# Cross-attention of a decoder layer: scores on four 32-row strips with dense keys, all 16 heads in one run

## The chip, the cores and the metric

The kernel runs on one core of a Trainium2 chip. Its engines are TensorE (PE; matmuls and their weight loads, which the profile shows as PEld), VectorE (DVE), ScalarE (ACT), GpSimd (POOL) and SyncE (SP, which issues most DMA transfers). The kernel keeps operands in SBUF, and PE's results go to PSUM, which the kernel divides into tiles of 128 partitions x 512 floats, a bank each; DVE and ACT read them from there.

The metric is the device time of one execution in microseconds (us), as the median of several runs.

## The reference

One decoder layer on `x` of shape (2, 2048, 512), in three parts, each added to its input and followed by a layer norm:

- a state-space mixer over the sequence (projections, a convolution of four taps, a scan in chunks, an output projection),
- cross-attention of 16 heads of 32 features over a context of 77 tokens for each of the two batches,
- a mixture of 16 slots: slots attend to all tokens (dispatch), each slot goes through its own expert (three matrices of 512 x 2048), and tokens attend to the slots (combine).

The middle part is what the change touches:

```python
q = (x @ q_w + q_b).reshape(B, T, H, D).transpose(0, 2, 1, 3)
k = (context @ k_w + k_b).reshape(B, S, H, D).transpose(0, 2, 1, 3)
v = (context @ v_w + v_b).reshape(B, S, H, D).transpose(0, 2, 1, 3)
att = jnp.einsum('bhtd,bhsd->bhts', q, k) / jnp.sqrt(jnp.float32(D))
causal = jnp.tril(jnp.ones((T, S), dtype=bool))
att = jnp.where(causal[None, None, :, :], att, -jnp.inf)
att = jax.nn.softmax(att, axis=-1)
y = jnp.einsum('bhts,bhsd->bhtd', att, v)
```

The causal mask matters only for the first 77 of 2048 tokens of a batch.

## The kernel before

The program has four stages, one after another, with little overlap between them. Times are of the profiled execution.

1. *Mixer* (0 to about 326 us): projections, convolution and scan. Beside it, in a generator called `setup`, the keys, values and a few folded matrices of the later stages are prepared, a step at a time, where the letter `U` stands in hand-tuned strings of letters (`TUNED["seq"]`).
2. *Attention* (about 326 to 912 us): 16 periods of 256 tokens (8 for each batch).
3. *Experts* (from about 912 us): 16 experts whose weights (192 pieces of 1 MB) stream from HBM through buffers in SBUF.
4. *Combine*: tokens attend to slots, last layer norm, output.

A period of the attention stage handles tokens 256 at a time, in two halves (`s`) of 128. Its pieces are small functions: `load`, `scaled`, `out_proj` (the mixer's output projection, residual and norm), `x1_transposed`, `queries` (in two halves of 256 features), `weigh` (scores and softmax of a group `hg` of four heads), `gather` (transposes the probabilities), `values` (probabilities times values), `o_proj` (output projection, residual, norm), `x2_transposed`, `dispatch`, `p_transposed` and `collect` (attention of the slots). Pieces of different periods are interleaved by a plan of eight steps for a period (`TUNED["plan"]`), where `W`, `G` and `V` stand for the next `weigh`, `gather` and `values`, with lists of their own for the stage's head and drain. That gives the order in which the source issues the work; when the program is built, a scheduler still moves instructions within each engine's queue, and the engines then run their queues in that fixed order.

Most matmuls work on numbers split into a high and a low part of a reduced float32 type (float32r, `FR`), three matmuls for a product: high x high, high x low, low x high. They are recorded by the helper `mm` (line 231); `split` makes the two parts (lines 234 and 242).

*Scores.* The features of four heads fill the 128 partitions, 32 each. The keys of a batch are laid out as block-diagonal matrices `kbh`, `kbl` of 128 x (4 heads x 77): in the columns of head `r` only its own 32 rows are not zero. So one matmul over all 128 rows gives the scores of four heads for 128 tokens, 128 x 308; three of them make a group. The result `sc` takes one PSUM bank, of two that take turns. `setup` writes the block-diagonal layout with four copies of 32 partitions each (`kf`, line 443), for each batch and each half of the features.

*Softmax.* For groups 1 and 3, DVE takes the maximum (line 810), subtracts it (line 811), ACT exponentiates, DVE sums (line 813). For groups 0 and 2, DVE takes the negated maximum (line 815) and ACT exponentiates four times with the maximum as bias and a running sum (line 818). DVE inverts the sum (line 819) and POOL scales (line 820).

*Values.* The probabilities `pp` are transposed on PE (line 828) into a bank `tr` and copied out to `pt`, of which there are three buffers. `values` multiplies: each head takes 32 columns of the PE array (77 rows x 32 columns), four heads side by side, and writes 32 partitions of the bank `y`, which is one bank of its own. Each float32 matmul of this kind is two records. After the fourth group, ACT and DVE split `y` into `yv`.

*PSUM in this stage.* `y` 1 bank, `mm` (projections, dispatch, collect) 2, `tr` (transposes) 2, `sc` 2.

Of the kernel before, what the change touches and what calls it, by code (L numbers as in the profile page):

```python
# [16 lines left out]
S = 77  # L17
NE, FF = 16, 2048
# [205 lines left out]
def tile_decoder(ctx, tc, a, out, dbg=None, upto=9, opt=None):  # L224
# [5 lines left out]
    def mm(o, l, r, start, stop, **kw):  # L230
        return pe.matmul(o, lhsT=l, rhs=r, start=start, stop=stop, **kw)  # L231
# [8 lines left out]
    def split(hi, lo, src, lo_eng=None, hi_eng=0):  # L240
        cp(hi_eng, hi, src)
        (lo_eng or dve).tensor_tensor(lo, src, hi, ALU.subtract)  # L242
# [38 lines left out]
    kbh, kbl = ([kv_[b].tile([128, 4, 4 * S], FR, name=f"kb{t}{b}") for b in range(B)] for t in "hl")  # L281
# [11 lines left out]
    with ExitStack() as st:  # L293
# [121 lines left out]
        def setup():  # L415
# [20 lines left out]
            for b in range(B):  # L436
                for h in range(2):
                    m2 = slice(2 * h, 2 * h + 2)
                    kf = sb.tile([128, 2, 4, S], FP, tag="sw", bufs=2, name="kf")
                    pool.memset(kf, 0.0)  # L440
                    for r in range(4):
                        sr = slice(32 * r, 32 * r + 32)
                        dve.tensor_copy(kf[sr, :, r, :], kst[sr, m2, b * S:b * S + S])
                    split(kbh[b][:, m2].rearrange("p m (r s) -> p m r s", s=S), kbl[b][:, m2].rearrange("p m (r s) -> p m r s", s=S), kf, pool)
                    yield
# [255 lines left out]
    with ExitStack() as st:  # L701
        psb = {tag: st.enter_context(tc.tile_pool(name="b_" + tag, bufs=n, space=PSUM, reuse_waits="tile"))
               for tag, n in (("y", 1), ("mm", 2), ("tr", 2), ("sc", 2))}
# [87 lines left out]
        def weigh(n, s, hg):  # L791
# [6 lines left out]
            qh, ql = ts[n]["q", hg // 2]  # L798
            h4 = slice(hg * 4, hg * 4 + 4)
            sc = PT("sc")  # L800
            for k, (l, r) in enumerate(((qh, kbh[b]), (qh, kbl[b]), (ql, kbh[b]))):
                mm(sc[:, 0:4 * S], l[:, hg % 2, ss], r[:, hg, :], k == 0, k == 2)
            sv = sc[:, 0:4 * S].rearrange("p (r s) -> p r s", s=S)
# [19 lines left out]
        def gather(n, s, hg):  # L823
            pp = ts[n].pop(("pp", s, hg))
            pt = sb.tile([S, 4, 128], FP, tag="pt", bufs=opt.get("pt", 3), name="pt")
            tp = PT("tr")
            for r in range(4):
                pe.transpose(tp[0:S, r * 128:r * 128 + 128], pp[:, r, :], ident)  # L828
            cp(EN.get('g%d' % hg, 1 - hg % 2), pt, tp[0:S, :].rearrange("p (r t) -> p r t", t=128))
            ts[n]["pt", s, hg] = pt  # L830

        def values(n, s, hg):
            b = n // NT
            if hg == 0:
                ts[n]["y", s] = PT("y", bufs=1)
            yp = ts[n]["y", s]
            pt = ts[n].pop(("pt", s, hg))
            for r in range(4):
                h = hg * 4 + r
                mm(yp[32 * r:32 * r + 32, hg * 128:hg * 128 + 128], vt[b][:, 32 * h:32 * h + 32], pt[:, r, :], True, True)  # L840
            if hg == 3:
                yh, yl = hi_lo("yv", [128, 4, 128], 1)
                split(yh, yl, ts[n].pop(("y", s)).rearrange("p (k t) -> p k t", t=128))
                ts[n]["yv", s] = (yh, yl)
# [106 lines left out]
        def needs(f, n, *a_):  # L951
# [9 lines left out]
            if f == "weigh":  # L961
                return [x("queries", a_[1] // 2)]
# [21 lines left out]
        if opt.get("drain"):  # L984
            dr_ = [tuple(o) for o in opt["drain"]]
            assert sorted(dr_) == sorted(ops[-len(dr_):])
            ops[-len(dr_):] = dr_
        for o in ops:
            assert all(d in done for d in needs(*o)), o
            assert o not in done  # L990
            done.add(o)
            fns[o[0]](*o[1:])
# [602 lines left out]
```

## Time and profile before

| | us |
|---|---|
| median of 3 runs (lowest to highest) | 1508.82 (1508.0 to 1513.46) |
| the profiled execution, its time | 1504.8 |
| its span | 1502.8 |
| PE busy | 1348.9 (90%) |
| DVE busy | 910.4 (61%) |
| ACT busy | 616.5 (41%) |
| POOL busy | 447.6 (30%) |

| operation of the attention stage | count | us each |
|---|---|---|
| one of three score matmuls, 128 x 308, record | 384 | 0.30 to 0.39 |
| maximum of a group of scores, DVE | 128 | 0.465 |
| subtracting it, DVE | 64 | 0.468 |
| exponential of one head, ACT, and reading its sum | 256 | 0.327 and 0.207 |
| transposing one head's probabilities, record | 512 | 0.273 |
| a pass of one head's values, record | 1024 | 0.273 |
| copy of transposed probabilities, ACT or DVE | 96, 32 | 0.582, 0.676 |
| splitting `y`, ACT, DVE | 32, 32 | 0.586, 0.691 |

How to read it: a record of PE lasts from the start of a matmul to the modelled end of its pipeline, and the next one starts long before. What a matmul costs its neighbours is the distance from its start to the next start. The views by stretch give the busy time of each engine between two moments; the view of the chain follows the work that ended last back from the end, each step to what released it. L231 is the line of the helper that records every matmul, so PE rows are told apart by the tiles that they write and read. In lines of PE, `128*32` is rows times columns of the weights, and `77x128` the moving operand.

### The profile page before, as it was taken

Reading aid. Unit: us, or ns where it says so; the run is one execution under the profiler, and the core shown is the slowest. Engines: PE = TensorE matmul, PEld = TensorE weight load, DVE = VectorE, ACT = ScalarE, POOL = GpSimd, SP = SyncE. Lnnn points to the kernel's source line nnn. Section 1 sums busy time; section 2 is a strip of 40 time slices with the busy share of each in tenths; the row PEclk is TensorE's granted clock in tenths of the full one; section 3 lists DMA queues with packets and bytes.
Section 4 is the critical chain, followed back from the end, with each engine's and each line's share of the span. In section 5 each row is a group of like instructions: output and inputs, shape, how many; then the busy total and the mean of one; then the engine's idle time right before and its main releaser. Section 6 shows DMA issues by size and latency. Waiting matters only on the chain.

```text
span 1502.8 us, 27725 instructions
## 1 busy us (share of the span) xinstructions
PE 1348.9 (90%) x10442; PEld 992.5 (66%) x10442; DVE 910.4 (61%) x2142; ACT 616.5 (41%) x1683; POOL 447.6 (30%) x496
## 2 busy tenths in 40 slices
PE   7899999988999999999999997858978778889896
PEld 6788889867888888888888874205644534533364
DVE  7997997857778888888887763102211111115597
ACT  5534544525655666565665551101100010105456
POOL 4634543645434444444443311000000000000054
PEclk9999999989999999999999997969999798999998
DMA  9889978993221222322210258999999999999447
GB/s 321 209 198 240 229 200 212 239 282 93 71 57 57 64 57 57 92 71 62 59 37 15 71 179 354 387 415 377 418 419 418 418 419 419 418 421 417 160 157 250
DMA packets 188061, 339.64 MB, mean 226 GB/s; under 512 B 12347, under 2 KB 135739, under 8 KB 163096
## 3 DMA queue, kind: packets, MB, share of 16 engines
q1 hardware_dynamic: 171632, 311.25, 59.9%
q10 hardware_dynamic: 16296, 26.62, 5.1%
q8 instruction: 83, 1.36, 0.4%
q14 instruction: 50, 0.41, 0.1%
HBM read 299.56 MB, written 38.27 MB: 225 GB/s over the span
## 4 chain that ended last, share of the span: by engine, by line
PE 58%; DVE 17%; DMA 17%; ACT 4%; issue 3%; POOL 1%; SPq 1%; ACTq 0%; POOLq 0%; DVEq 0%
PE mm L231 27%; DMA ew<-in_e_W 9%; PE up L231 6%; DMA ew<-in_e_Wg 6%; PE pj L231 5%; PE tr L828 4%; DVE X L530 3%; PE sc L231 3%; PE y L231 2%; PE yac L231 2%; PE gp L231 1%; PE uu L231 1%; DVE C L530 1%; PE tr L721 1%; DMA ut<-Ud 1%
## 5 line engine op out<-in xcount | busy, mean ns | idle before, releaser
L231 PE MATMUL up<-ew,hT 128*32 128x512 f32 x944 | 133.5, 637 | 33.0 <-DMA ew<-in_e_W 30.2
L820 POOL TENSOR_TENSOR pp<-pp,den 128x308 f32<-128x308 f32 x128 | 89.5, 704 | 156.8 <-DVE den L819 104.8
L1176 ACT ACTIVATE sv<-up 128x512 f32<-128x512 f32 x32 | 19.1, 597 | 270.2 <-PE up L231 260.5
L1185 POOL MEMSET aT<- 128x512 f32 x16 | 8.3, 525 | 401.2 <-PE yac L231 399.5
L231 PE MATMUL mm<-xTh,cqh 128*128 128x256 f32 x256 | 76.2, 309 | 31.2 <-ACT xTh L234 31.2
L1235 DVE TENSOR_TENSOR Qc<-mm,vec 128x512 f32<-128x512 f32 x32 | 22.1, 692 | 130.8 <-PE mm L231 125.3
L242 DVE TENSOR_TENSOR xTl<-tr,xTh 128x512 fp32r<-128x512 f32 x32 | 21.3, 688 | 113.3 <-ACT xTh L234 113.3
L231 PEld LDWEIGHTS up<-ew,hT 128*32 128x32 f32 x944 | 26.4, 112 | 94.4 <-issue 56.5
L828 PE MATMUL tr<-cst,pp 128*77 128x128 f32 x512 | 81.0, 282 | 2.0 <-DVE x1Tl L724 1.4
L234 ACT COPY pt<-tr 77x512 f32<-77x512 f32 x96 | 55.6, 582 | 63.2 <-PE tr L828 35.4
L231 PEld LDWEIGHTS mm<-xTh,cqh 128*128 128x128 f32 x256 | 51.4, 207 | 44.8 <-ACT xTh L234 34.7
L818 ACT ACTIVATE pp<-sc,mx 128x77 f32<-128x77 f32 x240 | 75.4, 327 | 11.1 <-DVE mx L815 10.3
L231 PE MATMUL mm<-xTl,cqh 128*128 128x256 f32 x256 | 77.6, 305 | 1.7 <-DVE xTl L242 1.7
L231 PE MATMUL mm<-x1Th,w30h 128*128 128x256 f32 x256 | 76.0, 298 | 2.7 <-ACT x1Th L723 1.5
L231 PE MATMUL mm<-xTh,cql 128*128 128x256 f32 x256 | 75.0, 295 | 0.0
L231 PE MATMUL mm<-x1Tl,w30h 128*128 128x256 f32 x256 | 73.8, 288 | 0.7 <-DVE x1Tl L724 0.7
L231 PE MATMUL mm<-x1Th,w30l 128*128 128x256 f32 x256 | 73.4, 287 | 0.0
L828 PEld LDWEIGHTS tr<-cst,pp 128*77 128x77 f32 x512 | 59.8, 148 | 16.7 <-issue 10.3
L530 DVE SCALAR_TENSOR_TENSOR X<-raw,vec,X 128x256 f32<-128x256 f32 x80 | 66.4, 876 | 5.4 <-ACT X L526 4.9
L231 PE MATMUL yac<-ew,aT 128*32 128x512 f32 x488 | 60.4, 631 | 5.8 <-issue 5.1
L746 POOL TENSOR_TENSOR ut<-ut,fb 128x512 f32<-128x512 f32 x32 | 41.3, 1292 | 76.9 <-DMA ut<-Ud 40.9
L231 PEld LDWEIGHTS mm<-xTl,cqh 128*128 128x128 f32 x256 | 52.0, 203 | 17.6 <-issue 14.2
(376 smaller groups left out, 4307.8 us busy)
## 6 DMA issues: line engine op xcount, KB each, us to landing
ew<-in_e_W SPq DMA_DIRECT2D x119, 1024.0 KB, 15.9
ew<-in_e_Wg SPq DMA_DIRECT2D x60, 1024.0 KB, 13.6
BS<-scrBc SPq DMA_DIRECT2D x48, 256.0 KB, 5.2
CS<-scrC SPq DMA_DIRECT2D x48, 256.0 KB, 6.4
xs<-in_xT SPq DMA_DIRECT2D x32, 256.0 KB, 5.7
xt<-in_x SPq DMA_DIRECT2D x32, 256.0 KB, 2.8
ut<-Ud SPq DMA_DIRECT2D x32, 256.0 KB, 3.5
fb<-fd SPq DMA_DIRECT2D x128, 64.0 KB, 3.1
```

What stands on the lines that cost most here:

```text
L231: return pe.matmul(o, lhsT=l, rhs=r, start=start, stop=stop, **kw)
L234: (act.copy, dve.tensor_copy, pool.tensor_copy)[e](o, i)
L242: (lo_eng or dve).tensor_tensor(lo, src, hi, ALU.subtract)
L530: dve.scalar_tensor_tensor(dst, raw[:, j, 1 + t:1 + t + TB], w4[:, t:t + 1], dst, ALU.mult, ALU.add)
L721: pe.transpose(tp[:, k * 128:k * 128 + 128], src[:, k * 128:k * 128 + 128], ident)
L746: (act, dve, pool)[EN.get('uf', 1)].tensor_tensor(ut, ut, fb, ALU.mult)
L818: act.activation(pp[:, r, :], sv[:, r, :], AF.Exp, bias=mx[:, h:h + 1], accum_out=den[:, h:h + 1])
L820: (act, dve, pool)[EN.get('d%d' % hg, 2)].tensor_tensor(pp, pp, den[:, h4].unsqueeze(2).to_broadcast([128, 4, S]), ALU.mult)
L828: pe.transpose(tp[0:S, r * 128:r * 128 + 128], pp[:, r, :], ident)
L1176: last["silu"] = act.activation(sv, up, AF.Silu)
L1185: pool.memset(aT, 0.0)
L1235: dve.tensor_tensor(Qc[b][:, mp * 2:mp * 2 + 2, t1:t1 + TB], qq, vec[:, V_CQ + mp * 2:V_CQ + mp * 2 + 2].unsqueeze(2).to_broadcast([128, 2 ...
```

## The change

- The keys are stored densely: for a batch, 128 partitions x 4 groups x 80 columns (77 and three of padding, `SP = 80`), 32 partitions a head, with no zeros around. `setup` fills them with one copy for each batch and has two steps fewer.
- The scores of a group come from four matmuls side by side in place of one, each over a strip of 32 rows (one head), 80 columns wide. Strip `r` of every group writes into bank `r` of a tile of four PSUM banks, at column `g * 80`. So a product of a group is 4 x 3 = 12 matmuls in place of 3.
- All 16 heads of 128 tokens are multiplied at once, 48 matmuls, when the first group's `weigh` comes. The other three `weigh` only do the softmax. The tile of four banks has one buffer.
- `values` does nothing for groups 0 to 2 and all 16 heads at group 3. Its result takes a bank of the projections (`mm`), and the bank `y` is gone. `pt` has six buffers in place of three.
- `weigh` needs both halves of the queries, and a loop puts every `weigh` of earlier tokens ahead of the first of later ones.

PSUM in this stage is then `mm` 2 banks, `tr` 2, `sc` 4.

```diff
+SP = 80
...
-    kbh, kbl = ([kv_[b].tile([128, 4, 4 * S], FR, name=f"kb{t}{b}") for b in range(B)] for t in "hl")
+    kbh, kbl = ([kv_[b].tile([128, 4, SP], FR, name=f"kb{t}{b}") for b in range(B)] for t in "hl")
...
             for b in range(B):
-                for h in range(2):
-                    m2 = slice(2 * h, 2 * h + 2)
-                    kf = sb.tile([128, 2, 4, S], FP, tag="sw", bufs=2, name="kf")
-                    pool.memset(kf, 0.0)
-                    for r in range(4):
-                        sr = slice(32 * r, 32 * r + 32)
-                        dve.tensor_copy(kf[sr, :, r, :], kst[sr, m2, b * S:b * S + S])
-                    split(kbh[b][:, m2].rearrange("p m (r s) -> p m r s", s=S), kbl[b][:, m2].rearrange("p m (r s) -> p m r s", s=S), kf, pool)
-                    yield
+                kf = sb.tile([128, 4, SP], FP, tag="sw", bufs=2, name="kf")
+                pool.memset(kf, 0.0)
+                dve.tensor_copy(kf[:, :, 0:S], kst[:, :, b * S:b * S + S])
+                split(kbh[b], kbl[b], kf, pool)
+                yield
...
-               for tag, n in (("y", 1), ("mm", 2), ("tr", 2), ("sc", 2))}
+               for tag, n in (("mm", 2), ("tr", 2))}
+        scp = st.enter_context(tc.tile_pool(name="b_sc", bufs=1, space=PSUM, reuse_waits="tile"))
...
             mx, den = ts[n]["mx", s]
-            qh, ql = ts[n]["q", hg // 2]
             h4 = slice(hg * 4, hg * 4 + 4)
-            sc = PT("sc")
-            for k, (l, r) in enumerate(((qh, kbh[b]), (qh, kbl[b]), (ql, kbh[b]))):
-                mm(sc[:, 0:4 * S], l[:, hg % 2, ss], r[:, hg, :], k == 0, k == 2)
-            sv = sc[:, 0:4 * S].rearrange("p (r s) -> p r s", s=S)
+            if hg == 0:
+                sc = ts[n]["sc", s] = scp.tile([128, 4, 512], FP, tag="sc", bufs=1, name="sc")
+                for g in range(4):
+                    qh, ql = ts[n]["q", g // 2]
+                    for k, (l, r_) in enumerate(((qh, kbh[b]), (qh, kbl[b]), (ql, kbh[b]))):
+                        for r in range(4):
+                            sr = slice(32 * r, 32 * r + 32)
+                            mm(sc[:, r, g * SP:g * SP + SP], l[sr, g % 2, ss], r_[sr, g, :], k == 0, k == 2)
+            sv = ts[n]["sc", s][:, :, hg * SP:hg * SP + S]
...
-            pt = sb.tile([S, 4, 128], FP, tag="pt", bufs=opt.get("pt", 3), name="pt")
+            pt = sb.tile([S, 4, 128], FP, tag="pt", bufs=opt.get("pt", 6), name="pt")
...
         def values(n, s, hg):
+            if hg < 3:
+                return
             b = n // NT
-            if hg == 0:
-                ts[n]["y", s] = PT("y", bufs=1)
-            yp = ts[n]["y", s]
-            pt = ts[n].pop(("pt", s, hg))
-            for r in range(4):
-                h = hg * 4 + r
-                mm(yp[32 * r:32 * r + 32, hg * 128:hg * 128 + 128], vt[b][:, 32 * h:32 * h + 32], pt[:, r, :], True, True)
-            if hg == 3:
-                yh, yl = hi_lo("yv", [128, 4, 128], 1)
-                split(yh, yl, ts[n].pop(("y", s)).rearrange("p (k t) -> p k t", t=128))
-                ts[n]["yv", s] = (yh, yl)
+            yp = PT("mm")
+            for g in range(4):
+                pt = ts[n].pop(("pt", s, g))
+                for r in range(4):
+                    h = g * 4 + r
+                    mm(yp[32 * r:32 * r + 32, g * 128:g * 128 + 128], vt[b][:, 32 * h:32 * h + 32], pt[:, r, :], True, True)
+            yh, yl = hi_lo("yv", [128, 4, 128], 1)
+            split(yh, yl, yp.rearrange("p (k t) -> p k t", t=128))
+            ts[n]["yv", s] = (yh, yl)
...
             if f == "weigh":
-                return [x("queries", a_[1] // 2)]
+                return [x("queries", 0), x("queries", 1)]
...
+        for n in range(N):
+            for s_ in range(2):
+                at_ = ops.index(("weigh", n, s_, 0))
+                for o in [x for x in ops[at_:] if x[0] == "weigh" and (x[1], x[2]) < (n, s_)]:
+                    ops.remove(o)
+                    ops.insert(at_, o)
+                    at_ += 1
```

## The prediction

> **What bounds the kernel now.** I read the page first, then busy time by stage, then the chain that ended last inside the attention stage, then the TensorE records one by one around the operations that change.
>
> Busy time by stage (columns: stretch, length, then busy time of PE, weight loads, DVE, ACT, POOL, granted clock, DMA share, GB/s):
>
> ```profile
> 326.00:420.00 94.00, 85.39 (x616) 72.20 (x615) 74.60 (x185) 51.84 (x177) 45.92 (x45) 0.95 0.38 115
> 420.00:860.00 440.00, 436.41 (x3371) 370.20 (x3370) 356.21 (x952) 265.74 (x890) 186.93 (x196) 1.00 0.20 59
> 860.00:912.00 52.00, 46.13 (x345) 35.52 (x343) 32.65 (x97) 26.33 (x79) 11.25 (x14) 0.98 0.56 205
> 912.00:1502.00 590.00, 484.70 (x3392) 253.21 (x3392) 174.77 (x475) 119.34 (x249) 48.22 (x64) 0.91 0.91 367
> ```
>
> Nearly all of the change lies in the attention stage, 326 to 912 us. In its steady part TensorE (PE) is busy 436 of 440 us at full clock, DVE 81%, ACT 60%. Since pipelined matmuls make "busy" too kind, the chain must confirm it. Between 520 and 562 us the chain is PE alone, in this order (start, length, group):
>
> ```profile
> 523.29 2.30 PE mm L231 x10
> 525.60 0.36 PE y L231 x8
> 525.95 0.59 PE tr L828 x4
> 526.54 0.43 PE sc L231 x3
> 526.98 0.44 PE tr L721 x4
> ...
> 545.47 0.79 PE y L231 x24
> ...
> 560.65 0.35 PE y L231 x8
> ```
>
> From 525.60 to 560.65 is one period of 35.05 us (256 tokens; 16 periods), with no wait for another engine in it. So a microsecond more or less of PE work in this stage is a microsecond of the kernel, and work of other engines is free until it becomes late.
>
> The same chain shows what a change of array shape costs. y (the values) runs on strips of 32 columns, tr and sc on the whole array. One y group (four matmuls, eight records) takes 0.36, three together 0.79, so a group is 0.216 of work and a first one has 0.14 more. The transposes after it take 0.59 instead of 0.44, another 0.15. **A visit to strips costs 0.29 us beyond its work.** The PE records show where:
>
> ```profile
> 603.08 0.28 PE L231 MATMUL mm<-x1Tl,w30h 128*128 128x256 f32 x1
> 603.20 0.28 PE L231 MATMUL mm<-x1Th,w30l 128*128 128x256 f32 x1
> 603.32 0.60 PE L721 MATMUL tr<-cst,x 128*128 128x128 f32 x4
> 603.85 0.42 PE L231 MATMUL y<-pt,vt 77*32 77x128 f32 x8
> 604.20 0.66 PE L828 MATMUL tr<-cst,pp 128*77 128x128 f32 x4
> ```
>
> Four transposes start at 603.32 and need 0.44; y starts at 603.85, so 0.09 of nothing lies before it. Another 0.09 lies behind it, and each side pays a first weight load that nothing covers. The weight queue's waits say the same: it stood with no releaser named
>
> ```profile
> PEld y L231 <- issue: 10.7, 41, 0.4
> PEld tr L828 <- issue: 8.5, 43, 0.2
> ```
>
> The third reading is what a short matmul costs:
>
> ```profile
> 250.10 1.85 PE L231 MATMUL qp<-sqTs,dwq 128*128 128x16 f32 x16
> 251.81 0.36 PE L231 MATMUL op<-cs,cst 128*128 128x1 f32 x2
> ...
> 150.32 0.66 PE L231 MATMUL gp<-CS,BS 96*128 96x128 f32 x4
> 150.82 0.33 PE L231 MATMUL pj<-xh,wi1h 128*128 128x256 f32 x1
> ```
>
> Sixteen qp matmuls with 16 moving columns start within 251.81-250.10 = 1.71 us, 0.107 each: 128 columns of weights set the pace, not the moving columns. gp, in the scores' number type with 128 columns, takes 0.50/4 = 0.125 with its first load.
>
> **The change, part by part.**
>
> *Scores, streaming.* Before: 16 periods x 24 = 384 matmuls of 308 columns, 0.43/3 = 0.143 each, 54.9 us. After: 384 groups of four strips, each strip 32 rows, 128 weight columns, 80 moving columns. No row shows row strips. Lower bound of a group: 0.107 to 0.111, the weight load, with the four side by side. Upper bound: one after another, 4 x 0.107 = 0.43. Column strips are the nearest row: the eight y records of a group fit in 0.36, which four serial ones could not. I take 0.111: 42.6 us, **-12.3**.
>
> *Visits.* Before: y in 104 visits (the scheduler joined some of the 128 groups), 104 x 0.29 = 30.2 us. After, in the order the changed program is built in, values take 78 visits, but the scores are not one run: the scheduler cuts them between projections and transposes into 121 visits, and 34 times goes directly from scores to values or back. A score visit has two changes of shape like y's, plus 0.08 for a first load of 128 rather than 32 weight columns, minus 0.07 since its last group, counted at 0.111, streams only 80 columns (80/256 of 0.12): 0.30. Sum 78 x 0.29 + 121 x 0.30 - 34 x 0.15 (one change shared) = 53.8; **+23.6**. Bounds of a score visit: 0 (row strips next to whole-array work need no gap) and 0.45.
>
> "TensorEngine Tiling (Array Packing)" of the Trainium skill, Key Properties, says that any change of tiling mode drains the array; y shows it for column strips, no row shows it for row strips. "TensorE: Matmul & The Clock Gate" there, Measured speedup vs the span model, gives 3.07 times for four row strips; by that a group would be 4 x 0.143/3.07, an estimate of 0.186, and the sum would be 29 us higher.
>
> *One score tile over four banks, single buffer.* A run now waits until all four softmax groups of the last one are read. In the built order 8.4 to 10 us of PE work lie between the runs. Reading needs on DVE four maxima (0.465) and two subtractions (0.468), 2.8 us, and on ACT eight exponentials with sums (0.327+0.207), 4.3 us. The whole softmax is 8.8 us of DVE and 10.4 of ACT in a period, so other work holds about 81-25 = 56% of DVE and 60-30 = 30% of ACT, and these reads need about 6.4 and 6.1 us: covered, with 2 us to spare. If that cover goes, PE stands with the projections queued behind the scores.
>
> *Values in the projections' two banks.* 32 more tiles take turns there. A next projection now waits for a split of the values: ACT 0.586, then DVE 0.69. In the built order most reuse has 2 us of PE work in front; one, the first output projection of a period behind the last collect, has 1.1 us against a DVE read of 0.7 plus its queue. For both bank edits: between 0 and 1.5 us a period; I take 0.3, near 0 since the covers are mostly longer than the chains, **+5**. The six pt buffers end ACT's wait for y (24.9 us in the steady part), off the path: nothing.
>
> *Setup.* 16 kf copies (8.0 us of DVE, two of them 2.46 and 2.34) become two; ACT loses half of 2.8 us of casts, POOL half of 8.7. The generator has two steps fewer, so the weight loads behind it (v_w, d_Wq, d_WkT, on SP's queue) and their matmuls and the POOL memset move forward past projection work. The two long copies lie on the chain, 4.8 us: gain between 0 (the new, wider copies wait as long) and 5, with 3 either way from the moved SP loads; I take **-3**.
>
> *After the stage.* Smaller tiles let five expert loads instead of four be issued at its start, but before had its fifth at 836 us; 1 MB at 418 GB/s is 2.4 us either way: 0.
>
> Sum: -12.3+23.6+5-3 = +13 (rounded). The profiled execution took 1504.8 us (span 1502.8), so 1518; the median of the runs, 1508.8, lies 4 above it, so I predict **1522**.
>
> **The rivals.**
>
> *Row strips change shape for free (faster).* Place: the 121 score visits. Then -12.3 - 7.6 (values, 26 visits fewer) - 3 + 2 of waits = -21: 1488. It decides from a score visit under 0.30 - 13/121 = 0.19 us. For it: shapes with the full 128 columns may not need what column strips need. Against: both gaps around y, on every visit.
>
> *Strips not side by side.* In pairs, 0.215 a group: 384 x 0.104 = +40, 1562. All serial: +122, 1644. For it: every strip loads 128 weight columns, y's only 32. Against: the y group.
>
> *PE waits for the softmax.* At 1 us in each of 32 runs, 32 in place of 5: 1549. It starts once the last group's maximum is over 2 us late in DVE's queue. Against: DVE's 19% idle.
>
> *The next stage swallows it.* From 912 us DMA is busy 91%; if the expert loads don't wait for the end of the attention, its length is hidden: about 1509. Against: they start at 836 to 925 us, as its buffers come free.
>
> **How the numbers follow.** Chances: the forecast 0.58 (1508 to 1540), free row strips 0.13, serial strips 0.09, softmax waits 0.12, swallowed 0.08. The range leaves out serial strips beyond pairs and what lies past free strips: 1486 to 1563. About 0.5%, 7.5 us, is what a measurement can tell from no change. Faster: 0.13 plus 0.03 from the forecast's low edge, 0.16; same: 0.08 swallowed and 0.11 of the forecast below 1516, 0.19; slower 0.65.
>
> **What would show it.** In the after profile: PE busy throughout 420 to 860 and a period near 36 us; score groups of about 0.11 when several stand together; gaps of 0.09 on both sides of each score visit; sc waits on ACT or DVE small; mm waits on the values' split under 0.5 us. Wrong if a score visit costs under 0.2, a group over 0.2, or PE shows waits of a microsecond before sc.

## The result, and the profile after

The changed kernel takes 1663.1 us (median of 4 runs, 1660.3 to 1667.8), the kernel before on the same chip 1511.1 (1508.0 to 1517.0): 1.101 times as long, 95% interval 1.0985 to 1.1032. The forecast was 1522 with a range to 1563: the sign holds, the size is off by more than ten times, +152 us against +13.

Busy time by stretch of the changed kernel (the bounds are set by hand; stretch, length, then PE, weight loads, DVE, ACT, POOL, granted clock, DMA share, GB/s):

```profile
0.00:320.00 320.00, 287.14 (x2646) 253.77 (x2646) 259.72 (x411) 148.82 (x280) 145.76 (x170) 0.94 0.89 228
420.00:1000.00 580.00, 513.95 (x4397) 420.64 (x4396) 371.10 (x983) 284.97 (x921) 191.35 (x198) 0.91 0.15 45
1062.00:1658.00 596.00, 489.27 (x3401) 254.96 (x3399) 176.84 (x486) 121.14 (x255) 48.25 (x64) 0.92 0.90 365
```

Taken between the same events of both profiles: the first transposes of x, with which the attention stage's own work begins, start at 334.7 us instead of 327.2. From there to the last matmul of `collect` it takes 737 us instead of 590, and what follows takes 587 instead of 586. So nearly all of the loss lies in the attention stage. Before, PE was busy 436 of 440 us there at full clock; now it is busy 514 of 580, and the clock granted is 0.91. A period of 256 tokens takes 46 us instead of 35.4.

What PE waited for in that stretch (total us, times, longest; the weight loads, PEld, wait for the same things):

```profile
PEld tr L831 <- POOL pp L823: 39.1, 27, 2.3
PE tr L831 <- POOL pp L823: 30.8, 24, 2.1
PEld mm L232 <- ACT pt L235: 24.6, 15, 2.4
PE mm L232 <- ACT pt L235: 20.7, 10, 2.2
PEld sc L232 <- issue: 15.9, 72, 0.4
POOL pp L823 <- DVE den L822: 116.3, 63, 17.9
```

The transposes of the softmax weights wait for their normalisation on GpSimd, the values for the copies of those transposes. GpSimd in turn waits for the inverted sums of VectorE (the last line). Scores hardly wait for their tile: their own line names no releaser and is 0.2 us for each of 72 waits, as at the changes of shape around y before, and the scores' other waits in this stretch add up to 0.6 us. What that looks like on PE (start, length, group; in brackets the idle time before it and who ended it):

```profile
717.48 0.60 PE L719 MATMUL tr<-cst,x 128*128 128x128 f32 x4
718.01 0.31 PE L232 MATMUL sc<-kbh,qh 32*128 32x80 f32 x4
718.15 0.29 PE L232 MATMUL sc<-kbl,qh 32*128 32x80 f32 x4
718.26 0.29 PE L232 MATMUL sc<-kbh,ql 32*128 32x80 f32 x4
718.37 0.29 PE L232 MATMUL sc<-kbh,qh 32*128 32x80 f32 x4
...
721.69 1.14 PE L831 MATMUL tr<-cst,pp 128*77 128x128 f32 x4 [2.15 <-POOL pp L823]
722.62 1.06 PE L719 MATMUL tr<-cst,x 128*128 128x128 f32 x4
```

Two readings. The strips do what they were priced at: each group of four starts 0.11 us after the last, the four side by side. And a wait of 2.15 us stands before the transposes at 721.69, after which the same four transposes of x that took 0.60 at 717.48 take 1.06 at 722.62: the granted clock is 0.5 from 720.8 to 727.7 us.

To split the period I went through PE's records from the third to the twelfth dispatch, nine periods. What a start-to-start distance has beyond the time that the two shapes need (0.109 up to 128 columns, 0.12 for 256, 0.226 for 512, 0.097 more at a change of shape) counts as a wait if it is over 0.15 us; of what remains in stretches with clock 0.5, half counts as the clock's price; the rest is PE's own work.

| us a period | period | own work | waits | price of the clock | time at half clock |
|---|---|---|---|---|---|
| before | 35.4 | 35.2 | 0.2 | 0 | 0 |
| after | 46.0 | 36.1 | 6.2 | 3.8 | 8.8 |

The own work grew by 0.9 us a period; the prediction had (-12.3+23.6)/16 = 0.7. That is some 14 us of the 152. The waits, 6 us a period, and the clock, 3.8, are the result. (16 times 10.6 is 170 us, more than the 147 that the stage lost, since its first and last periods lost less.)

How the waits come about shows in one half, 128 tokens. Before, here is a half's first group: its first and last product, its maximum, its gather:

```profile
664.14 0.30 PE L231 MATMUL sc<-kbh,qh 128*128 128x308 f32 x1
664.42 0.30 PE L231 MATMUL sc<-kbh,ql 128*128 128x308 f32 x1
665.26 0.46 DVE L815 TENSOR_REDUCE mx<-sc 128x4 f32<-128x308 f32 x1
678.48 0.60 PE L828 MATMUL tr<-cst,pp 128*77 128x128 f32 x4
```

In the changed kernel, PE, at the run's beginning and end and at the gathers that follow:

```profile
734.98 0.31 PE L232 MATMUL sc<-kbh,qh 32*128 32x80 f32 x4
...
736.97 0.31 PE L232 MATMUL sc<-kbh,ql 32*128 32x80 f32 x4
...
753.25 0.29 PE L232 MATMUL sc<-kbh,ql 32*128 32x80 f32 x4
...
757.76 0.60 PE L831 MATMUL tr<-cst,pp 128*77 128x128 f32 x4
...
762.26 0.66 PE L831 MATMUL tr<-cst,pp 128*77 128x128 f32 x4 [1.40 <-POOL pp L823]
763.59 0.50 PE L232 MATMUL mm<-w31h,yyh 128*128 128x512 f32 x1 [0.67 <-DVE Z L924]
```

and VectorE meanwhile:

```profile
754.45 0.46 DVE L818 TENSOR_REDUCE mx<-sc 128x4 f32<-128x308 f32 x1
...
756.54 0.45 DVE L813 TENSOR_REDUCE mx<-sc 128x4 f32<-128x308 f32 x1
...
757.34 0.47 DVE L814 TENSOR_TENSOR pp<-sc,mx 128x308 f32<-128x308 f32 x1
757.73 0.46 DVE L818 TENSOR_REDUCE mx<-sc 128x4 f32<-128x308 f32 x1
758.12 0.68 DVE L857 TENSOR_TENSOR zt<-mm,x 128x512 f32<-128x512 f32 x1
...
758.78 0.46 DVE L816 TENSOR_REDUCE den<-pp 128x4 f32<-128x308 f32 x1
759.16 0.73 DVE L924 SCALAR_TENSOR_TENSOR Z<-Z,al,mm 128x512 f32<-128x512 f32 x1
...
761.20 0.23 DVE L822 RECIPROCAL den<-den 128x4 f32<-128x4 f32 x2
761.35 0.44 DVE L813 TENSOR_REDUCE mx<-sc 128x4 f32<-128x308 f32 x1
```

The first group's scores are ready at 737.3, but the run's last only at 753.5: half of them need the second query projection, and projections lie between. The first maximum starts at 754.45, behind the run's last matmul, because in the built program it waits for the whole tile. Then the four groups' maxima and subtractions come within 10 us, mixed with residual sums, normalisation and the update of Z, all in VectorE's one queue, and each waits for the one before it: the sum of the second group is done at 759.24, its inverse stands behind that other work until 761.20, then comes GpSimd's scaling, and then the gather of 762.26, for which PE has stood still for 1.40 us. Over 13 halves in the steady part the first maximum came on average 2.2 us after a half's first score before the change and 11.2 after it (some 17 in the first half of a period, whose run is torn apart, and 5 in the second); the first gather at 17.9 and 15.0. So a first group's softmax had 15.7 us until its gather, and now has 3.8, which is about what it takes.

### The profile page after: what moved, and what is told of

Same layout as the page of the kernel before. It is cut to its first block, busy times and chain, and to the rows that moved or that the text cites. A ratio compares the mean times of both kernels' runs of the same rounds, so it can differ in the third digit from the quotient of the medians.

```text
span 1658.5 us, 30033 instructions
## 1 busy us (share of the span) xinstructions
PE 1431.0 (86%) x11594; PEld 1043.7 (63%) x11594; DVE 902.6 (54%) x2128; ACT 627.3 (38%) x1681; POOL 444.2 (27%) x492
## 4 chain that ended last, share of the span: by engine, by line
PE 52%; DVE 21%; DMA 15%; ACT 6%; issue 3%; POOL 1%; SPq 0%; ACTq 0%; POOLq 0%; DVEq 0%
PE mm L232 24%; DMA ew<-in_e_W 10%; PE up L232 5%; PE pj L232 5%; DMA ew<-in_e_Wg 4%; PE tr L831 3%; PE yac L232 2%; ACT pp L821 2%; DVE X L527 2%; PE sc L232 2%; PE uu L232 2%; PE gp L232 2%; PE tr L719 1%; DVE bst L687 1%; DVE mx L813 1%
## 5 line engine op out<-in xcount | busy, mean ns | idle before, releaser
L232 PE MATMUL up<-ew,hT 128*32 128x512 f32 x944 | 135.1, 641 | 39.5 <-DMA ew<-in_e_W 34.9
L831 PE MATMUL tr<-cst,pp 128*77 128x128 f32 x512 | 93.6, 315 | 42.9 <-POOL pp L823 37.6
L831 PEld LDWEIGHTS tr<-cst,pp 128*77 128x77 f32 x512 | 70.3, 170 | 59.9 <-POOL pp L823 47.3
L243 POOL TENSOR_TENSOR yyl<-ut,yyh 128x512 fp32r<-128x512 f32 x32 | 41.2, 1289 | 228.5 <-PE sc L232 203.2
L232 PE MATMUL mm<-x1Th,w30h 128*128 128x256 f32 x256 | 87.2, 341 | 4.0 <-ACT x1Th L721 4.0
L232 PE MATMUL mm<-x1Tl,w30h 128*128 128x256 f32 x256 | 80.5, 314 | 0.2 <-DVE x1Tl L722 0.2
L232 PE MATMUL mm<-x1Th,w30l 128*128 128x256 f32 x256 | 79.8, 312 | 0.0
L232 PE MATMUL mm<-pt,vt 77*32 77x128 f32 x1024 | 47.7, 292 | 24.2 <-ACT pt L235 22.4
```

## The experiments

All times below are medians of at least 4 runs, compared with 7 to 12 runs of the kernel before on the same chip. Their split of the period, by the same reckoning:

| us a period | period | own work | waits | clock's price | time, us | ratio to before |
|---|---|---|---|---|---|---|
| e3 values in one place, projections' banks | 35.4 | 34.8 | 0.7 | 0 | 1515.1 | 1.0048 |
| e11 values in one place, own bank | 36.3 | 35.3 | 1.0 | 0 | 1521.3 | 1.0071 |
| e1 whole-array scores in one run | 39.5 | 35.0 | 3.6 | 0.9 | 1565.2 | 1.0367 |
| e5 the same, a tile for each group | 38.0 | 34.7 | 2.8 | 0.6 | 1543.0 | 1.0207 |
| e2 strips, a run for each group | 39.3 | 37.1 | 1.9 | 0.4 | 1579.4 | 1.0474 |
| e4 run given priority | 44.8 | 35.4 | 7.1 | 2.3 | 1653.5 | 1.0958 |
| e6 run whole, behind the queries | 42.6 | 34.5 | 5.3 | 2.8 | 1605.7 | 1.0615 |
| e7 gathers a step later | 41.2 | 36.1 | 3.2 | 1.9 | 1624.3 | 1.0726 |
| e8 e6 and e7 | 41.0 | 34.2 | 4.1 | 2.7 | 1594.1 | 1.0547 |
| e9 queries together | 43.4 | 35.8 | 4.6 | 3.1 | 1638.6 | 1.0844 |
| e10 whole runs, spread | 41.0 | 34.6 | 5.3 | 1.1 | 1599.3 | 1.0579 |
| e12 maxima in program order | 42.9 | 35.6 | 5.0 | 2.2 | 1632.0 | 1.0797 |
| e13 e10 in program order | 44.3 | 35.3 | 5.6 | 3.4 | 1653.8 | 1.0955 |
| e14 after, no maxima | 44.4 | 36.8 | 3.6 | 3.9 | 1634.6 | 1.0828 |
| e15 before, no maxima | 35.3 | 35.1 | 0.2 | 0 | 1498.8 | 0.9931 |
| e16 e10, no maxima | 37.6 | 34.7 | 2.9 | 0 | 1543.9 | 1.0233 |
| e17 after, waits filled | 43.1 | 39.2 | 3.0 | 0.9 | 1626.3 | 1.0762 |

### Which part of the change it is: e1 to e4

**e1**, the one run without strips (the values as in the changed kernel; the edit against the kernel before):

```
-            sc = PT("sc")
-            for k, (l, r) in enumerate(((qh, kbh[b]), (qh, kbl[b]), (ql, kbh[b]))):
-                mm(sc[:, 0:4 * S], l[:, hg % 2, ss], r[:, hg, :], k == 0, k == 2)
+            if hg == 0:
+                sc = ts[n]["sc", s] = scp.tile([128, 4, 512], FP, tag="sc", bufs=1, name="sc")
+                for g in range(4):
...
+                        mm(sc[:, g, 0:4 * S], l[:, g % 2, ss], r[:, g, :], k == 0, k == 2)
```

> Block-diagonal keys and whole-array matmuls as before, but the 16 heads of 128 tokens in one run into one tile of four banks, single buffer, group g in bank g; values as in the changed kernel. No strips for the scores, and no bank that two groups share. Shared banks (each group's scores lie in all four banks, so the first maximum waits for the last of the 48 matmuls): this kernel has none of it, so it stays near the kernel before, 1505 to 1545 us. One run with a single buffer as such: most of the 150 us remains, 1600 to 1665. Row strips: near before, too, so this run does not tell strips from shared banks. Values in the projections' banks: 1600 or more.

Measured 1565.2, interval of the ratio 1.0333 to 1.0401: neither. Over a third of the loss (57 of 152 us) is there with no strip and no shared bank. The theory of shared banks, as I put it, falls for that part: in this kernel, too, the first maximum mostly came 0.3 to 0.5 us behind the run's last matmul, since the wait goes by the tile, not by the bank.

**e2**, strips without the one run (against the changed kernel):

```
-                sc = ts[n]["sc", s] = scp.tile([128, 4, 512], FP, tag="sc", bufs=1, name="sc")
-                for g in range(4):
+            sc = scp.tile([128, 4, 512], FP, tag="sc", bufs=1, name="sc")
...
+                    mm(sc[:, r, 0:SP], l[sr, hg % 2, ss], r_[sr, hg, :], k == 0, k == 2)
```

> Dense keys and four row strips as in the changed kernel, but the scores of one group of four heads are a run of their own (12 matmuls into a tile of four banks, single buffer), issued where before had them; values as in the changed kernel. Row strips as such: the slowness stays, 1620 to 1670 us. Shared banks of four groups, or one run of all heads: the slowness goes but for the visits; in the built order 147 score visits x 0.30 + 87 value visits x 0.29 - 46 x 0.15 - 104 x 0.29 of before = +32, streaming -12, so about 1530, with waits of the single buffer for a group's maxima and exponentials up to 1570. Values in the projections' banks: 1600 or more.

Measured 1579.4 (1.0444 to 1.0504). Against e3, which has the same values, the own work is 37.1-34.8 = 2.3 us a period longer, 37 us in all. The prediction's prices give somewhat less: 147 visits x 0.30 + (87-67) x 0.29 - 46 x 0.15 (scores next to values, one change of shape shared) - 12.3 = 31. If the score visits alone make up the difference, one costs 0.34. The other 27 us are waits (1.9 against 0.7), clock (0.4) and a stage that begins 9 us later (335.3 against 326.4), less what the shorter periods at both ends save.

**e3**, the values alone (against the kernel before):

```
-            yp = ts[n]["y", s]
-            pt = ts[n].pop(("pt", s, hg))
+            if hg < 3:
+                return
+            yp = PT("mm")
+            for g in range(4):
+                pt = ts[n].pop(("pt", s, g))
```

> The kernel before with only the values changed: all 16 heads of 128 tokens behind the last gather, into the projections' two banks. If the values in the projections' banks are the cause, 1590 to 1665 us. If not, 1500 to 1520: 67 value visits instead of 104 x 0.29 = -11, with up to 0.3 us of waits in each of 32 splits, +10.

Measured 1515.1 (1.0029 to 1.0066): the own work falls by 0.4 us a period and the waits rise by as much. The values in the projections' banks are not what makes the changed kernel slow.

**e4**, the run given priority, fewer pieces:

```
-                for g in range(4):
+                with tc.high_priority():
+                    for g in range(4):
```

> The changed kernel with the 48 score matmuls of a run given priority in the order, so that fewer projections lie between them: 82 score visits instead of 121. If the tearing apart of the run is the cause (its last pieces come late, so the softmax starts late), at least half of the 150 us goes: 1530 to 1590. If shared banks, or the one run as such, are the cause, the softmax still comes in one burst: only visits go, 39 x 0.30 - 18 x 0.15 = -9, and some wait: 1620 to 1660.

Measured 1653.5 (1.0932 to 1.0984). Fewer visits, no fewer waits (7.1): as the second theory had it. A first half's run still took 16 us from first to last matmul, since it still began before the second query projection.

### Where the wait is made: e5 to e9

**e5**, e1 with a tile for each group:

```
-                sc = ts[n]["sc", s] = scp.tile([128, 4, 512], FP, tag="sc", bufs=1, name="sc")
                 for g in range(4):
+                    sc = ts[n]["sc", s, g] = scp.tile([128, 512], FP, tag="sc", bufs=4, name="sc")
```

> The whole-array run of e1, with one edit: the four groups of a run have a tile (one bank) each instead of parts of one tile, so a group's first maximum waits for its own three matmuls and not for the run's last. Theory of the whole run (the softmax of the first group starts only behind the run's last matmul, and PE then waits for it): e1's 3.6 us of waits and 0.9 us of lowered clock a period go, 1565 -> 1510 to 1530 us. Theory of the one run as such (scores of 16 heads issued in one place): stays at 1550 to 1570.

Measured 1543.0 (1.0168 to 1.0246), between the two. PE's waits for the softmax weights in e1 (450 to 850 us):

```profile
PEld tr L831 <- POOL pp L823: 34.4, 19, 3.2
PE tr L831 <- POOL pp L823: 22.4, 10, 2.9
```

and in e5:

```profile
PEld mm L231 <- ACT x1Th L724: 13.9, 9, 2.3
PEld mm L231 <- DVE Z L924: 11.7, 19, 1.4
PEld tr L831 <- POOL pp L823: 3.8, 5, 1.0
```

The wait that was named goes from 34.4 to 3.8 us: it does come from the softmax starting behind the whole run. But other waits take most of its place, and the sum only falls from 3.6 to 2.8 us a period: the query projections now wait for x1's transposes.

**e6**, the run behind the last query matmul; **e7**, gathers and values a plan step later; **e8**, both:

```
-                for g in range(4):
+                with tc.high_priority(), tc.issue_after(ts[n]["lq"]):
+                    for g in range(4):
```

> The changed kernel with the 48 matmuls of a run queued behind the last query projection and given priority: in the built order every run stands whole, 32 score visits instead of 121, with nothing between. PE's own work falls by 89 x 0.30 - 34 x 0.15 = 22 us. Theory of tearing (the first half's run takes 16 us because projections lie inside it): the waits at least halve too, 1560 to 1600 us. Theory of place (the softmax of all four groups still starts behind the run, and the gathers stand a step behind it): only the work goes, 1635 to 1650.

```
+        later(ops, "gather", 2)   # right behind the weigh two steps on, before: one
+        later(ops, "values", 3)
```

> The changed kernel with the gathers and the values of tokens 768 to 3071 (tiles 3 to 11 of 16) one plan step, about 4.4 us, later. Theory of place (PE waits because the gathers stand too close behind a softmax that begins after the whole run): waits fall from 6.2 to under 2.5 us a period and the clock with them, 1550 to 1610 us. If VectorE, ScalarE and GpSimd simply can't do the burst faster, or the late values now hold up the output projection: 1640 to 1680.

> e6 and e7 together. Theory of place: the work is 36.1 - 1.4 us a period and little waiting is left, 1500 to 1550 us. Theory of a burst that the other engines can't do in time: 1600 or more.

Measured 1605.7 (1.0577 to 1.0654), 1624.3 (1.0672 to 1.0781) and 1594.1 (1.0509 to 1.0584). The first two lie between the branches expected, the third just under its second one. In e6 every run took 1.3 us and stood whole, and the own work fell by 1.6 us a period as priced (1.4), below that of before. The waits only went from 6.2 to 5.3, and most of them are now for other things (3.5 for the transposes of x). e7 halves the waits, but not below the 2.5 that I had asked for. e8, where both suspected causes are gone, still waits 4.1 us a period.

**e9**, the second query projection directly behind the first:

```
+        for n in range(3, 15):
+            ops.remove(("queries", n, 1))
+            ops.insert(ops.index(("queries", n, 0)) + 1, ("queries", n, 1))
```

> The changed kernel with the second query projection of tiles 3 to 14 moved directly behind the first, one plan step earlier, and nothing else. The score visits stay 121. A run of the first half then ends earlier against its gathers: counted in PE work of the built order, the first gather stands 9.3 us (first half) and 8.2 us (second half) behind the run's end instead of 4.2 and 3.5, while the softmax of a first group took about 4 us from there and that of the last about 12. Theory of place (PE waits because the gathers stand too close behind a softmax that begins after the whole run): waits fall from 6.2 us a period to under 2 and the lowered clock goes with them, 1530 to 1590 us. If it is a burst that the other engines can't do in time: 1630 to 1665.

Measured 1638.6 (1.0823 to 1.0865). The gathers had twice the distance from the run, and the waits for the softmax weights fell from 3.1 to 1.0 us a period; the sum of the waits fell only to 4.6. So the gathers' place is where the waits show, not all of why they are there. In e9 a wait that the changed kernel hardly has comes in: by the same reckoning 1.9 us a period now stand before scores. The trace has

```profile
PE sc L232 <- DVE pp L814: 12.3, 8, 1.5
```

in 450 to 850 us, the subtraction on VectorE that reads the last run's scores. With the gathers out of the way, the single tile itself holds PE up for a part of the time, the wait that the prediction had asked about.

### Is it VectorE's queue: e10 to e16

**e10**, e9 with whole runs, 13 and 21 us apart (`lq` is the last query matmul, `lt` the last transpose of the first half's first gather):

```
+                with tc.high_priority(), tc.issue_after(ts[n].get(("lt", 0, 0), ts[n]["lq"]) if s else ts[n]["lq"]):
```

> e9 with whole runs: the first half's 48 matmuls queue behind the last query projection, the second half's behind the transposes of the first half's first gather, both with priority. In the built order 32 score visits, nothing inside a run, runs 13 and 21 us apart, first gathers 11 us behind the run's end. Theory of place: work of 34.2 to 34.5 us a period as in e6 and e8 and 0.5 to 1.5 us of waits, 1500 to 1535 us. If 32 rows' scores in one burst hold up the other engines' queues whatever the gathers' place, as in e6: 1570 to 1610.

Measured 1599.3 (1.0545 to 1.0612), the second branch. The own work is 34.6, the waits for the softmax weights are gone, and 5.3 us a period of waits remain. What PE waited for in e10, 450 to 850 us:

```profile
PEld mm L232 <- DVE zt L863: 21.0, 10, 2.6
PEld mm L232 <- DVE Z L930: 13.0, 17, 0.9
PEld tr L720 <- ACT pt L235: 12.8, 10, 1.6
PEld mm L232 <- ACT dth L235: 9.7, 10, 1.0
```

Residual sums, the update of Z, copies: work that has nothing to do with the scores, except that it stands in the same queues.

**e12** and **e13** keep the later groups' maxima at their own plan steps on VectorE, in the changed kernel and in e10 (there with the second half's run behind the third gather):

```
-                dve.tensor_reduce(mx[:, h4], sv, AX.X, ALU.max)
+                (tc.keep_in_program_order if hg else id)(dve.tensor_reduce(mx[:, h4], sv, AX.X, ALU.max))
```

> The changed kernel with one edit: the maxima of groups 1 to 3 of a half stay behind everything that VectorE was given before them in program order, so they come at their own plan steps. In VectorE's built order the four maxima of a half stand within 11 instructions in the changed kernel, 31 to 37 before the change; here 21 to 36. PE has 74 score visits instead of 121 and 96 value visits instead of 78: -47 x 0.30 + 18 x 0.29 = -9 us. Theory of the burst (four groups' softmax at once stand ahead of other work in the queues of VectorE, ScalarE and GpSimd, and PE waits for that work): waits fall from 6.2 us a period to under 3, 1560 to 1610 us. If the order on VectorE is not it (the run as such makes every chain late): 1640 to 1665.

> e10 with the same edit as e12, and the second half's run behind the transposes of the first half's third gather instead of its first. 32 score visits, 101 value visits, 20 and 14 us between the runs, first gathers 2.6 to 5.5 us and last gathers 15 to 23 us behind the run's end. Theory of the burst: waits fall from e10's 5.3 us a period to under 2, 1520 to 1560 us. Otherwise 1580 or more.

Measured 1632.0 (1.0776 to 1.0818) and 1653.8 (1.0926 to 1.0984). The first is a little better than the changed kernel and lies between its branches, the second is much worse than e10. That the four groups stand together on VectorE is not the cause by itself: spread out, the last group's maxima ended 19 to 21 us behind the run's first matmul (17.8 in the changed kernel, 8.1 in e10), and some 2 us a period of the waits in e12 and 3 in e13 are for gathers and values.

**e14** to **e16** take part of VectorE's load away. They leave out the maxima and their subtraction, which also takes a link out of the chain from the scores to the weights, in the changed kernel, in the kernel before and in e10:

```
-                dve.tensor_reduce(mx[:, h4], sv, AX.X, ALU.max)
-                dve.tensor_tensor(pp, sv, mx[:, h4].unsqueeze(2).to_broadcast([128, 4, S]), ALU.subtract)
-                act.activation(pp, pp, AF.Exp)
+                act.activation(pp, sv, AF.Exp)
```

> The changed kernel without the softmax's maxima and without their subtraction: the exponentials take the scores as they are, the sums and the division stay. VectorE loses 8 maxima of 0.45 and 4 subtractions of 0.47 a period, 5.5 of its 28.7 us, and a group's exponentials start as soon as the scores are there. The built order has 172 score visits instead of 121, +51 x 0.30 - 10 x 0.15 = +14 us of PE's own work. Theory of VectorE's queue (the chain of the changed kernel runs through VectorE for 34 of 140 us: residual sums, maxima, denominators, normalisation one behind the other while PE has nothing): waits fall from 6.2 us a period to 3 or less, the clock's cost from 3.7 to 1.5 or less, 1570 to 1610 us. If VectorE's load is not it: 1650 to 1690.

> The kernel before without the maxima and their subtraction, as in e14: the control. Both theories: PE sets the period there, VectorE is 81% busy beside it, so nothing but the order changes: 1495 to 1515 us.

> e10 (whole runs, 32 score visits, gathers 11 us behind the run) without the maxima and their subtraction. Theory of VectorE's queue: waits fall from 5.3 us a period to 2 or less, and with 34.5 us of work a period this is 1510 to 1545. If the waits are set elsewhere (ScalarE's or GpSimd's part of the softmax): 1580 or more.

Measured 1634.6 (1.0809 to 1.0846), 1498.8 (0.9908 to 0.9954) and 1543.9 (1.0208 to 1.0258). The control gains 12 us and its steady period is the same (35.3 against 35.4), as it must be where PE sets it. The two others gain 28 us, in spite of 14 us more for visits, and 55. Their waits fall from 6.2 to 3.6 and from 5.3 to 2.9: not quite to the 3 and 2 that I had asked for, but by 2.4 to 2.6 us a period where the control's stay at 0.2. In e16:

```profile
PEld tr L720 <- ACT pt L235: 14.8, 11, 1.7
PEld mm L232 <- ACT dth L235: 10.6, 11, 1.0
PEld mm L232 <- DVE Z L927: 10.1, 18, 0.8
PEld mm L232 <- DVE zt L860: 3.5, 11, 1.4
```

the 21.0 us for the residual sum have become 3.5; the waits for ScalarE's copies have stayed. The price of the clock in e16 is gone (granted clock 1.00 from 450 to 850 us), though 2.9 us of waits remain: none of them is over 1.7 us long. In e14 the clock stayed as it was (3.9): most of its waits are before gathers, eight in nine periods, of about 3 us each. In e10 PE didn't wait for the softmax weights any more, so what e16 gains is, as far as the waits tell, load taken from VectorE's queue; in e14 load and the shorter chain can't be told apart.

**e11**, e3 in its own bank (`yp = PT("y", bufs=1)`), was meant as a version faster than both:

> The kernel before with the values of 16 heads in one place, but in their own bank as before, not in the projections'. In the built order 98 value visits instead of 104, and 54 instead of 21 direct changes between scores or values: both whole-array here except the values, so 6 x 0.29 = 2 us less. 1500 to 1512 us; if e3's 7 us come from the shared banks, they are gone here; if from the values' later place, they stay, 1512 to 1520.

Measured 1521.3 (1.0055 to 1.0087), no faster than e3 (1.0029 to 1.0066). So a loss of this size needs no shared bank. Where the two lose it differs: e11 in the attention stage, which takes 602 us from the first transposes of x to the last matmul of `collect`, e3 behind it (592 there, against 590 before). What e3's 7 us come from isn't shown.

e15 is the one version that beats both kernels, by 0.7%. Without the maxima it is the same function only as long as no score is so large that its exponential overflows.

### Where the clock goes: e17

```
             tp = PT("tr")
+            if hg in (0,) and 2 <= n <= 13:
+                for j in range(6):
+                    mm(tp, wo_h[:, j % 4, 0:128], wo_h[:, j % 4, :], True, True)
```

> The changed kernel with six needless matmuls of 512 columns (0.226 us each, constant operands, into the bank that the transposes then overwrite) ahead of the first gather of every half of tiles 2 to 13: 144 x 0.226 = 32.5 us of added PE work, most of it just where PE waits for the first group's weights. The order changes a little, too: 134 score visits instead of 121, +13 x 0.30 - 14 x 0.15 = +2. Theory of the clock (a stretch in which PE stands still for over about 1.3 of 3.4 us is followed by one at half clock): the added work fills waits that are there anyway and less of the time is at half clock, 4 us or less instead of 8.8 a period, so the time falls in spite of the added work, 1625 to 1655 us. If the clock is lowered by something else than the waits: 1665 to 1700.

Measured 1626.3 (1.0725 to 1.0799). 32.5 us of needless matmuls made the kernel 37 us faster. The stretch from 450 to 850 us, first of the changed kernel, then of e17:

```profile
450.00:850.00 400.00, 353.20 (x3046) 290.44 (x3042) 256.62 (x674) 196.28 (x638) 135.56 (x139) 0.91 0.16 48
```

```profile
450.00:850.00 400.00, 378.47 (x3304) 310.01 (x3302) 269.09 (x720) 202.36 (x668) 146.17 (x149) 0.98 0.17 51
```

The clock goes from 0.91 to 0.98, its price from 3.8 to 0.9 us a period, and the waits from 6.2 to 3.0: the added 3.1 us of work lie where PE stood still.

## Why the prediction was right and wrong

**Right: what bounds the kernel before, and the prices of PE's own work.** Strips at 0.111 a group, side by side; 0.09 to 0.10 of nothing on both sides of a score visit; 0.30 for a visit, a little low: e2 has them together, 37 us measured and 31 by those prices. That answers two rivals. Free row strips (1488) fall, since a visit costs what was assumed, and so do strips one after another (1562, 1644). The estimate from "TensorE: Matmul & The Clock Gate" of the Trainium skill, 0.186 for a group, set the page's 3.07 against four whole-array matmuls of 308 columns; against four strips one after another, 0.43 in the prediction's own bound, the estimate would be 0.140, and 0.111 was measured. The drain at a change of mode that "TensorEngine Tiling (Array Packing)" states under Key Properties shows for row strips too, as the 0.09. The forecast's own reason for "slower" thus makes some 14 of the 152 us; that the other nine tenths have the same sign is luck.

**Right in size: values in the projections' banks** (0.3 us a period with the single tile; e3 has 0.5 of waits and 0.4 less work) **and what follows the stage**, put at 0: 587 us against 586. "The next stage swallows it" falls: it began 155 us later and was as long.

**Wrong, and small: the setup.** The term was -3; the first transposes of x come 7.5 us later, not earlier. The setup's last matmul does end earlier, at 274.6 us instead of 311.6, but the mixer's last one ends at 333.9 instead of 312.5, and from 288 to 335 us PE has 27 us at half clock instead of 15. All 13 kernels with dense keys start the attention at 328.2 to 335.3 us, all 6 with the old ones at 324.7 to 327.2. That the setup's matmuls are missing in the mixer's last stretch fits this, but wasn't tried by itself.

**Wrong: the step "covered, with 2 us to spare".** I asked whether the tile would be free for the next run, and compared 8.4 to 10 us of PE work between runs with 6.4 us of reading. That answer was right: PE hardly ever waited for the tile (0.6 us in 580; e9 shows what it looks like when it does). It was the wrong question. The run also moves the *start* of the softmax: from 2.2 us behind a half's first score to 11.2, since the first maximum now waits for the last of 48 matmuls, half of which need the second query projection. Nobody had to wait for the tile; PE waited for the weights and their transposes, two engines further on. The term was +5 for both bank edits; the waits measured are 6.0 us a period more, some 96 us. e5 shows, on whole-array scores, that this start is part of it (the wait for the weights 34.4 -> 3.8 us, and 22 us of time).

**The rival that came, undersized.** "PE waits for the softmax" named the right engines, with 1 us for each of 32 runs; it was 3 us. But its condition, too, was the tile (a last maximum that is late), and its sign was waits before sc; the waits came before the gathers and the values. Against it I held VectorE's 19% idle. An idle share says nothing of when: from 756.5 to 764 us in the lines above VectorE has one piece of work behind another and PE stands for 1.40 and 0.67 us; with the maxima and subtractions gone from VectorE, e14 and e16 lose about 2.5 of the 5 to 6 us of waits a period (the control, with the same edit, has nothing to gain there).

**Missing: the clock.** The prediction had no term for it, since the steady part of before ran at 1.00. Its 3.8 us a period are some 60 of the 152 us. e17 shows that it follows from the waits, and e1 (no strips, 0.9) and e16 (strips, 0) that it needs no strips, and that strips alone don't bring it.

**Open.** 2.9 to 3.6 us a period of waits are left when VectorE is relieved, and each move of the run, the gathers or the softmax (e6 to e13) brought waits of other kinds. Even e11, which only moves the values, costs 10 us. What the changed kernel waits beyond e1, 2.6 us a period, goes with a longer run in the first halves, 13.5 to 18.3 us against 9.8; but e6 and e10, with runs of 1.3 us, still wait 5.3, so the length alone doesn't explain it. Nor does GpSimd: in the changed kernel it stands still for 15 us and more in most periods until a score matmul comes (`yyl`, 203 us in 12 waits from 420 to 1000 us), but in e10 it doesn't, and PE's waits are still there. It also fits that the order written out for the kernel before suits its own small groups and no other, and that every queue behind it is in order, but I have not shown this: no order was made anew for the changed kernel.

## What to carry to other kernels

When small pieces of work are joined into one run, don't only ask whether the run's buffer comes free in time; ask when the first consumer can start, and count from there to whoever waits last. In a kernel where PE is busy 99% of the time with full clock, price a wait of about 2 us at more than its length: in the changed kernel the clock added 60% to the waits, in e16, with short ones only, nothing. And a wait that goes away in one place (e5, e9, e10) shows nothing until the time has gone, too.

## What the runs showed of the hardware

**The clock follows the last 3.41 us.** The changes of the granted clock in these traces lie on a grid of 3.41 us. Over 16 profiled kernels (the changed one, e1, e2, e4 to e14, e16, e17), from 430 to 850 us, I took each such window at full clock and summed PE's idle time in it by its records. Under 0.5 us idle: followed by a window at half clock in 0 of 1378 cases. 0.5 to 1.0: 18 of 195. 1.0 to 1.5: 21 of 80. 1.5 to 1.9: 37 of 48. From 1.9 us on: 48 of 48. "TensorE: Matmul & The Clock Gate" of the Trainium skill (HAM oscillation) puts the rule as no idle gaps over about 3.4 us; here idle time of 1.9 us within 3.41 was always enough, and no wait in the nine periods of the changed kernel is longer than 2.3 us.

**Four row strips beat the whole array on short products, changes of shape aside.** A group of four strips of 32 rows with 128 weight columns and 80 moving ones takes 0.111 us, the same scores by one whole-array matmul with 308 columns 0.143.
